# Taylor attention on one Trainium2 core: q's columns of two groups of heads in one projection, and the scores' constant one added by GpSimd instead of sums of values

## The chip, the core and the metric

The kernel runs on one core of a Trainium2 chip. The metric is the device time of one execution in microseconds (us). The kernel before took 3826.05 us, the median of three runs (3818.64 to 3838.03). Engines are named as the profile names them: PE (TensorE, matmuls; PEld is its weight load), DVE (VectorE), ACT (ScalarE), POOL (GpSimd), SP (SyncE, which issues the DMAs). SBUF is the memory that all engines work in, PSUM the one that PE writes to.

## What is computed

Two sublayers, each wrapped as x + LN(sublayer(LN(x))), in fp32, on x of shape 8 x 512 x 128 (8 batches, 512 tokens, 128 features). The change concerns the first sublayer, attention with 16 heads, 16 features per head for q and k and 64 for v, whose weights are a Taylor polynomial of second order in place of an exponential:

```python
def taylor_exp(x):
    x2 = (x[..., :, None] * x[..., None, :]).reshape(*x.shape[:-1], FEATURE_DIM * FEATURE_DIM) / R2
    return jnp.concatenate([ones, x / RRD, x2 / RD], axis=-1)
qf, kf = taylor_exp(q), taylor_exp(k)
A_qk = jnp.tril(jnp.einsum('bhnd,bhmd->bhnm', qf, kf))     # causal
y = jnp.einsum('bhnm,bhme->bhne', A_qk, v)
rms = jax.lax.rsqrt(jnp.mean(y * y, axis=-1, keepdims=True) + RMS_EPS)
y = y * rms * g_weight                                      # per head
out = y.transpose(0, 2, 1, 3).reshape(b, l, NUM_HEADS * HEAD_DIM) @ Wo.T
```

With s = q.k the weight is 1 + s/4 + s*s/32. Twice that is (1 + s/4)^2 + 1, and as y is normalised, the factor of two is taken up by the epsilon. The second sublayer is a stack of six layers of windowed attention and a gated feed-forward; nothing of it is changed.

## The kernel before

The program is one unrolled stream. PE's order is the order of the code (a manual schedule for PE); the other engines are ordered by a scheduler that works with priorities, and buffers come from pools with a fixed number of slots for each tag, so an instruction that writes a slot waits until the slot's last reader is done.

The Taylor attention comes first. Per batch there are 4 groups of 4 heads, and per group 3 steps (`STEPS`), which take the key blocks of 128 tokens as [0], [1] and [2, 3]; only queries from the block on are computed (512, 384, and 256 + 128 columns). `slot(k)` (L361) emits the work of step k: the scores of step k, then one of head norm, projection of q and k, or projection of v for a neighbouring group, once per batch some work on the next or last batch, and last the weighted sum of step k - 2.

- `project_qk` (L234): the 4 heads of a group have 16 features of q each, padded with 16 zero columns to 32 rows, so that every head stands in its own 32 rows of 128. Two matmuls of 128x512 (q and k), each copied out of PSUM by ACT (L240).
- `squares` (L260): per key block 4 matmuls (L270), one per head, each on its 32 rows of k and q, into two PSUM tiles; ACT squares them with bias 1 and scale 1/4 into `am` (L279). On the diagonal block of 128x128 alone, DVE adds one and multiplies by the causal mask `keep` (L283). Off the diagonal the one is not added.
- `in_by_features` (L211) makes the columns of x's normalised batch and, from the same PSUM tile, the running sums of x over the blocks before each block (`cb`, L221 to L223). `sums_before` (L226) multiplies them by v's weights: 8 matmuls of 128x4 (L230), copied by DVE to `vs` (L232). That is the sum of v over all earlier blocks, which is what a constant one off the diagonal adds to y.
- `weigh` (L289): y += v * am (L300) in one PSUM tile that has a single slot; after a group's last step DVE adds `vs` to y while it copies it out to `yT` (L308), and ACT squares that (L313).
- `head_norm` (L316) forms the mean squares with a matmul (`ms`, L321), and `attn_out` (L331) projects a batch's result (`po`, L336), normalises it and adds it to x, the sum on POOL (L345).

`am` lives in the tags `qk` and `v2`, two slots each; q and k in the tag `pe`; the scores in PSUM's tag `mm` (two slots, both taken by one step); projections, `ms`, `vs` and transposes share PSUM's tag `tr` (two slots). Then 192 units of the second sublayer follow, each 128 tokens of a batch in one layer. Before `by_keys` in every fourth of them from the sixth on (t = 5), `nc.tensor.addr_align(128, offset=IN_STEP)` (L747) pads PE's instruction stream with NOPs up to place 98 of 128.

Of the kernel before, what the change touches and what calls it, by code (L numbers as in the profile page):

```python
# [8 lines left out]
F32 = mybir.dt.float32  # L9
BF16 = mybir.dt.bfloat16  # L10
AF = mybir.ActivationFunctionType
ALU = mybir.AluOpType
AX = mybir.AxisListType
PSUM = bass.MemoryType.PSUM

P = 128
DM = 128
H = 16
FD = 16
HD = 64  # L20
# [8 lines left out]
def sandwich_kernel(ctx: ExitStack, tc: tile.TileContext, ins: dict, out: bass.AP):  # L29
    nc = tc.nc  # L30
    x_d = ins["L0_attn_hidden_states"]
    B, N, _ = x_d.shape
    NB = N // P
# [44 lines left out]
    def transposed(ps, src, rows, cols):  # L78
        nc.tensor.transpose(ps[:cols, :rows], src, ident[:rows, :rows])  # L79
# [58 lines left out]
    psum = ctx.enter_context(tc.tile_pool(name="psum", bufs=2, space=PSUM))  # L138
    wl = ctx.enter_context(tc.tile_pool(name="wl", bufs=2))
    f2 = ctx.enter_context(tc.tile_pool(name="f2", bufs=2))  # L140
    f3 = ctx.enter_context(tc.tile_pool(name="f3", bufs=3))
    f1 = ctx.enter_context(tc.tile_pool(name="f1", bufs=1))

    HF = HD // 2
    NP = H // 2
# [5 lines left out]
    def load_x(b):  # L151
        t = f2.tile([P, NP, W + P], F32, tag="kT", name=f"xin_{b}")
        xin[b] = t.rearrange("p a b -> p (a b)")[:, : NB * DM].rearrange("p (n d) -> p n d", d=DM)
        nc.sync.dma_start(xin[b], x_d[b].rearrange("(n p) d -> p n d", p=P))


    tw = wl.tile([P, 3, 2, 512], F32, tag="wqkv", name="tw")
# [6 lines left out]
    wqk = tw[:, 0]  # L164
    wvT = tw[:, 1].rearrange("p s c -> p (s c)")
# [28 lines left out]
    for qd in range(4):  # L194
        r = slice(qd * W, (qd + 1) * W)
# [6 lines left out]
    bt = [dict() for _ in range(B)]  # L202
    gr = [dict() for _ in range(NG)]
# [7 lines left out]
    def in_by_features(b):  # L211

        xl = bt[b].pop("xl")
        ps = psum.tile([P, NB, P], F32, tag="tr", name="tr")
        for j in range(NB):
            transposed(ps[:, j, :], xl[:, j, :], P, P)
        bt[b]["xlT"] = xlT = f2.tile([P, N], F32, tag="ge", name=f"xlT_{b}")
        nc.scalar.copy(xlT, ps.rearrange("p a b -> p (a b)"))
        cb = f2.tile([P, NB], F32, tag="cb", name=f"cb_{b}")
        nc.vector.memset(cb[:, 0:1], 0.0)  # L220
        nc.vector.tensor_reduce(cb[:, 1:NB], ps[:, : NB - 1, :], AX.X, ALU.add)  # L221
        for j in range(2, NB):
            nc.vector.tensor_tensor(cb[:, j : j + 1], cb[:, j : j + 1], cb[:, j - 1 : j], ALU.add)  # L223
        bt[b]["cb"] = cb

    def sums_before(b):  # L226

        ps = psum.tile([P, NP, NB], F32, tag="tr", name="vs")
        for c in range(NP):
            nc.tensor.matmul(ps[:, c, :], wvT[:, c * P : (c + 1) * P], bt[b]["cb"], start=True, stop=True)  # L230
        bt[b]["vs"] = vs = f2.tile([P, NP, NB], F32, tag="vs", name=f"vs_{b}")
        nc.vector.tensor_copy(vs, ps)  # L232

    def project_qk(G):  # L234
        b, g = divmod(G, NQ)
        gr[G]["qk"] = qk = f2.tile([P, 2, N], F32, tag="pe", name=f"tqk_{G}")
        for s in range(2):
            ps = psum.tile([P, N], F32, tag="tr", name="qk")
            nc.tensor.matmul(ps, wqk[:, s, g * P : (g + 1) * P], bt[b]["xlT"], start=True, stop=True)  # L239
            nc.scalar.copy(qk[:, s], ps)  # L240

    def project_v(G):
        b, g = divmod(G, NQ)
# [9 lines left out]

    STEPS = [[0], [1], [2, 3]]
    steps = [(G, s) for G in range(NG) for s in range(len(STEPS))]

    def squares(k):  # L260

        G, s = steps[k]
        qk = gr[G]["qk"]
        sc = [psum.tile([P, 2, N], F32, tag="mm", name="sc") for _ in range(2)]
        at_, places = 0, []
        for m in STEPS[s]:
            n = N - m * P
            for h in range(4):
                r = slice(32 * h, 32 * h + 32)
                nc.tensor.matmul(  # L270
                    sc[h // 2][:, h % 2, at_ : at_ + n],
                    qk[r, 1, m * P : (m + 1) * P], qk[r, 0, m * P :], start=True, stop=True,
                    skip_group_check=True,
                )
            places.append((m, at_, n))
            at_ += n
        am = f2.tile([P, 4, 512], F32, tag=("qk", "v2")[k % 2], name="am")
        for i in range(2):
            nc.scalar.activation(  # L279
                am[:, 2 * i : 2 * i + 2, :at_], sc[i][:, :, :at_], AF.Square, bias=1.0, scale=0.25  # L280
            )
        for m, o, n in places:
            nc.vector.scalar_tensor_tensor(  # L283
                am[:, :, o : o + P], am[:, :, o : o + P], 1.0,
                keep.unsqueeze(1).to_broadcast([P, 4, P]), ALU.add, ALU.mult,
            )
        gr[G]["am", s] = am, places

    def weigh(k):  # L289

        G, s = steps[k]
        b, g = divmod(G, NQ)
        if s == 0:
            gr[G]["y"] = psum.tile([P, 2, N], F32, tag="s", name="y", bufs=1)
        y, v = gr[G]["y"], gr[G]["v"]
        am, places = gr[G].pop(("am", s))
        for m, o, n in places:
            for h in range(4):
                r = slice(HD * (h % 2), HD * (h % 2 + 1))
                nc.tensor.matmul(  # L300
                    y[r, h // 2, m * P :], v[:, m, h * HD : (h + 1) * HD], am[:, h, o : o + n],
                    start=(m == 0), stop=(m == NB - 1), skip_group_check=True,
                )
        if s == len(STEPS) - 1:
            yT = f2.tile([P, 2, NB, P], F32, tag="sq", name="yT")
            with tc.high_priority():
                for i in range(2):
                    nc.vector.tensor_tensor(  # L308
                        yT[:, i], y[:, i].rearrange("p (n m) -> p n m", m=P),
                        bt[b]["vs"][:, 2 * g + i, :].unsqueeze(2).to_broadcast([P, NB, P]), ALU.add,  # L310
                    )
            ysq = f2.tile([P, 2, N], F32, tag="t1", name="ysq")
            nc.scalar.activation(ysq, yT.rearrange("p a n m -> p a (n m)"), AF.Square)  # L313
            gr[G]["yT"], gr[G]["ysq"] = yT, ysq

    def head_norm(G):  # L316
        yT, ysq = gr[G].pop("yT"), gr[G].pop("ysq")
        rs = f2.tile([P, 2, N], F32, tag="t2", name="rs")
        for i in range(2):
            ps = psum.tile([P, N], F32, tag="tr", name="ms")  # L320
            nc.tensor.matmul(ps, same, ysq[:, i], start=True, stop=True)  # L321
            ln = nc.scalar.activation(rs[:, i], ps, AF.Ln, bias=eps4, scale=1.0 / HD)
            issue_behind(ln, tables[-1])
        exps.append(nc.scalar.activation(rs, rs, AF.Exp, scale=-0.5))
        gr[G]["yn"] = yn = f1.tile([P, 2, N], F32, tag=("qT", "pT", "on", "oT")[G % NQ], name="yn")
        nc.vector.scalar_tensor_tensor(
            yn.rearrange("p a n -> p (a n)"), yT.rearrange("p a n m -> p (a n m)"), gw,
            rs.rearrange("p a n -> p (a n)"), ALU.mult, ALU.mult,
        )
# [31 lines left out]
    def slot(k):  # L361

        G, ph = divmod(k, len(STEPS))
        b, g = divmod(G, NQ)
        if k < len(steps):
            squares(k)
        if ph == 0 and 0 <= G - 2 < NG:
            head_norm(G - 2)
        if ph == 1 and G + 1 < NG:
            project_qk(G + 1)  # L370
        if ph == 2 and G + 1 < NG:
            project_v(G + 1)
        if g == 0 and ph == 1 and b + 1 < B:
            norm_in(b + 1)
        if g == 1 and ph == 0 and b + 1 < B:
            in_by_features(b + 1)
        if g == 1 and ph == 1 and b + 1 < B:
            sums_before(b + 1)
        if g == 1 and ph == 2 and b >= 1 and k < len(steps):
            attn_out(b - 1)  # L380
        if g == 2 and ph == 2 and b >= 1 and k < len(steps):
            to_state(b - 1)
        if 0 <= k - 2 < len(steps):
            weigh(k - 2)
# [339 lines left out]
    with tc.manual_schedule(engines={mybir.EngineType.PE}):  # L724
        norm_in(0)
        in_by_features(0)
        project_qk(0)
        project_v(0)
        sums_before(0)
        layers[0] = load_layer(0)  # L730
        for k in range(len(steps) + 2):
            slot(k)
# [83 lines left out]

def _attn_weights(given):

    import numpy as np

    parts = []
    for nm in ("Wq", "Wk"):
        w = given[f"L0_attn_{nm}"].reshape(H, FD, DM)
        parts.append(np.pad(w, ((0, 0), (0, FD), (0, 0))).reshape(2 * FD * H, DM).T)
    parts.append(given["L0_attn_Wv"].T)
    parts.append(given["L0_attn_Wo"].T.reshape(H // 2, P, DM).transpose(1, 0, 2).reshape(P, H // 2 * DM))
    return np.ascontiguousarray(np.concatenate(parts, 1))


# [39 lines left out]
```

## Time and profile before

| | |
|---|---|
| median of three runs | 3826.05 us |
| the profiled execution | 3825.62 us |
| its span, first to last instruction | 3823.9 us |
| granted PE clock, mean | 0.994 of full |
| PE busy | 3703.6 us, 97% |
| DVE, ACT, POOL busy | 73%, 70%, 48% |
| Taylor attention, with its start | about 0 to 535 us |
| scores' squares on ACT (L279), 128x1024 and 128x768 | 1.02 and 0.80 us each |
| masked add on DVE (L283) | 0.69 us each |
| q and k records on PE (L239) | 128, the shortest 0.59 us |
| records of the sums of values on PE (L230) | 128, 0.25 us each |

The page gives for each engine its busy time and for each group of equal instructions the number, the busy time, the mean duration of one, and the idle time ahead of them with what ended it. Matmuls overlap each other in the pipeline, so the time that a block of them takes on PE is read from the timeline, from its start to the next block's start, and not from the sum of its records. A line "A <- B" under the idle time names the instruction whose end released the waiting one.

### The profile page before, as it was taken

The page shows a single profiled execution, that of the slowest core. Times are in us where ns is not written, and L with a number is a line of the kernel's source. Part 1 is how long each engine was busy: PE and PEld are TensorE (multiplying, and loading weights), DVE is VectorE, ACT ScalarE, POOL GpSimd, SP SyncE. Part 2 cuts the span into 40 slices and gives each one's busy share as a digit, 9 for nine tenths or more (in the row PEclk, how much of TensorE's full clock was granted, in tenths as well). Part 3 has the DMA queues.
Part 4 walks back from the last instruction along what each step waited for, and adds up shares of the span by engine and source line. Part 5 has one row for each costly group of instructions (what it writes and reads, how often), then busy time and mean ns, then how long its engine had stood idle before and what let it go on. Part 6 is the DMA issues. An engine that isn't in the chain of part 4 may idle for free.

```text
span 3823.9 us, 152697 instructions
## 1 busy us (share of the span) xinstructions
PE 3703.6 (97%) x65600; PEld 2456.2 (64%) x65600; DVE 2794.7 (73%) x4308; ACT 2662.9 (70%) x6750; POOL 1842.6 (48%) x1311
## 2 busy tenths in 40 slices
PE   8999999999999999999999999999999999989997
PEld 4545556666666666666666666666666666666664
DVE  4555567787877778787777778777777878777774
ACT  5565557777777777777777777777777777767665
POOL 0000025555555555555555655555555555555552
PEclk9999999999999999999999999999999999999998
DMA  2000012222232222322222322223222222222221
GB/s 82 17 9 12 6 51 72 60 67 62 73 79 69 66 58 66 81 73 62 67 66 58 88 72 67 57 67 82 71 65 65 67 58 65 65 67 69 64 67 32
DMA packets 153219, 233.66 MB, mean 61 GB/s; under 512 B 32622, under 2 KB 53356, under 8 KB 151788
## 3 DMA queue, kind: packets, MB, share of 16 engines
q1 hardware_dynamic: 152556, 223.89, 22.8%
q8 instruction: 530, 8.68, 0.9%
q14 instruction: 133, 1.09, 0.1%
HBM read 24.54 MB, written 4.19 MB: 8 GB/s over the span
## 4 chain that ended last, share of the span: by engine, by line
PE 95%; issue 2%; ACT 2%; DVE 1%; POOL 0%; DMA 0%; POOLq 0%; SPq 0%; DVEq 0%; ACTq 0%
PE tr L79 20%; PE mm L439 17%; PE py L627 9%; PE mm L497 9%; PE po L598 8%; PE sp L558 8%; PE y L300 4%; PE mm L652 3%; PE mm L654 3%; PE py L687 3%; PE sc L270 3%; PE sp L551 2%; PE vv L248 2%; PE qk L239 1%; PE po L336 1%
## 5 line engine op out<-in xcount | busy, mean ns | idle before, releaser
L470 POOL TENSOR_TENSOR qk<-t,t 128x1024 f32<-128x1024 f32 x384 | 909.9, 2370 | 679.3 <-DVE t L454 405.3
L486 POOL TENSOR_TENSOR qk<-qk,ss 128x1024 f32<-128x1024 f32 x384 | 722.2, 1902 | 16.0
L439 PE MATMUL mm<-wqkv,state 128*128 128x512 f32 x1536 | 698.4, 597 | 2.6 <-ACT v L502 2.6
L447 DVE TENSOR_TENSOR t<-mm,tab 128x512 f32<-128x512 f32 x768 | 498.6, 671 | 239.5 <-PE mm L439 239.5
L570 ACT ACTIVATE pe<-sp,mx 128x64 f32<-128x64 f32 x3072 | 652.1, 381 | 2.3 <-DVE mx L566 2.3
L462 ACT ACTIVATE sq<-mm 128x512 f32<-128x512 f32 x768 | 421.3, 607 | 118.6 <-DVE t L454 114.0
L454 DVE TENSOR_TENSOR t<-mm,tab 128x1024 f32<-128x1024 f32 x384 | 468.4, 1220 | 5.9
L439 PEld LDWEIGHTS mm<-wqkv,state 128*128 128x128 f32 x1536 | 273.7, 191 | 289.6 <-issue 242.2
L473 DVE TENSOR_REDUCE ss<-sq 128x16 f32<-128x1024 f32 x384 | 448.6, 1209 | 0.7 <-ACT sq L462 0.6
L79 PE MATMUL tr<-ident,qk 128*128 128x128 f32 x3072 | 440.7, 276 | 1.8 <-ACT qT L536 0.8
L536 ACT COPY kT<-tr 128x512 f32<-128x512 f32 x384 | 225.6, 587 | 299.6 <-PE tr L79 299.4
L79 PEld LDWEIGHTS tr<-ident,qk 128*128 128x128 f32 x3072 | 351.0, 141 | 120.7 <-issue 100.8
L627 PE MATMUL py<-oT,wo 128*128 128x128 f32 x3072 | 377.4, 276 | 0.5 <-ACT oT L620 0.5
L627 PEld LDWEIGHTS py<-oT,wo 128*128 128x128 f32 x3072 | 364.5, 194 | 0.7 <-ACT oT L620 0.7
L497 PE MATMUL mm<-wqkv,state 128*128 128x512 f32 x768 | 363.1, 595 | 0.3 <-ACT sq L462 0.3
L620 ACT COPY oT<-tr 128x512 f32<-128x512 f32 x384 | 206.8, 589 | 221.5 <-PE tr L79 218.9
L598 PE MATMUL po<-v,pT 64*32 64x64 f32 x24576 | 301.9, 225 | 56.0 <-PE tr L79 49.1
L598 PEld LDWEIGHTS po<-v,pT 64*32 64x32 f32 x24576 | 274.2, 105 | 98.0 <-PE tr L79 88.5
L566 DVE TENSOR_REDUCE mx<-sp 128x16 f32<-128x1024 f32 x192 | 235.1, 1225 | 104.2 <-PE sp L558 104.2
L558 PE MATMUL sp<-kT,qT 64*32 64x64 f32 x24576 | 304.7, 226 | 6.4 <-issue 6.4
L558 PEld LDWEIGHTS sp<-kT,qT 64*32 64x32 f32 x24576 | 270.6, 105 | 62.5 <-issue 60.0
L606 DVE TENSOR_TENSOR on<-po,su 128x1024 f32<-128x1024 f32 x192 | 235.2, 1225 | 96.8 <-PE po L598 96.8
(114 smaller groups left out, 5082.8 us busy)
## 6 DMA issues: line engine op xcount, KB each, us to landing
v<-v SPq DMA_DIRECT2D x1152, 128.0 KB
v<-v SPq DMA_DIRECT2D x672, 64.0 KB
wqkv<-in_L_ffn_Wqkv_dram SPq DMA_DIRECT2D x6, 1536.0 KB
wo<-in_L_ffn_Wo_dram SPq DMA_DIRECT2D x6, 512.0 KB
xin<-_attn_hidden_states_dram SPq DMA_DIRECT2D x8, 256.0 KB
xr<-_attn_hidden_states_dram SPq DMA_DIRECT2D x8, 256.0 KB
x<-xr SPq DMA_DIRECT2D x8, 256.0 KB
xr<-x SPq DMA_DIRECT2D x8, 256.0 KB
```

What stands on the lines that cost most here:

```text
L79: nc.tensor.transpose(ps[:cols, :rows], src, ident[:rows, :rows])
L439: nc.tensor.matmul(ps[:, a].rearrange("p h d -> p (h d)"), lhs, wqkv[:, s, a, :], start=True, stop=True)
L447: nc.vector.tensor_tensor(t2[:, a], ps[:, 1 - a], tab[:, 2 * s + 1, j, HF * a : HF * (a + 1)].unsqueeze(1).to_broadcast([P, H, HF]), ALU.mult,
L454: nc.vector.tensor_tensor(t1, ps, tab[:, 2 * s, j, :].rearrange("p (a d) -> p a d", a=2).unsqueeze(2) .to_broadcast([P, 2, H, HF]), ALU.mult,)
L470: nc.gpsimd.tensor_tensor(qk[:, s].rearrange("p h a d -> p a h d"), t1, t2, ALU.add)
L473: su = nc.vector.tensor_reduce(u["ss"][:, s], u["sq", s].rearrange("p h a d -> p h (a d)"), AX.X, ALU.add)
L486: nc.gpsimd.tensor_tensor(t, t, ss[:, i, :].unsqueeze(2).to_broadcast([P, H, HD]), ALU.mult)
L497: nc.tensor.matmul(ps[:, p, :], lhs, L["wqkv"][:, 2, p, :], start=True, stop=True)
L558: nc.tensor.matmul(sp[W * w : W * (w + 1), p, pair, :], qT[HD * p : HD * (p + 1), pair, W * w : W * (w + 1)], kT[HD * p : HD * (p + 1), pa ...
L570: ex = nc.scalar.activation(pe[:, pair, p, :], sp[:, p, pair, :], AF.Exp, bias=mx[:, p, pair : pair + 1])
L598: nc.tensor.matmul(po[W * w : W * (w + 1), p, pair, :], pT[r, pair, W * w : W * (w + 1)], v2[r, w, HD * pair : HD * (pair + 1)], start=Tru ...
L627: nc.tensor.matmul(py, L["wo"][:, c, :], oT[:, c, :], start=(c == 0), stop=(c == NP - 1))
```

## The change

Three things are changed, all in the Taylor attention.

1. **q packed.** The rows of a q projection are no longer padded with zeros: 128 rows hold 8 heads, two in each 32 rows, and serve two groups. The zeros are now in k's weights: k of a group has its head's 16 rows in one half of its 32 and zeros in the other, so the product picks the right head. q is projected for even groups only, into a new pool `fq` with two slots, and the odd group uses the same tile. The heads are taken in another order (`heads`), for Wv and Wo too; their shapes stay.
2. **No sums of values.** `cb`, `sums_before` and `vs` go. After the last step DVE copies y out as one instruction of 128x1024.
3. **The one added to the scores.** Off the diagonal POOL adds 1.0 to the squares in place, behind ACT: 4 heads x 384, 256 and 128 columns for the key blocks 0, 1 and 2, one instruction each. DVE's masked add on the diagonal stays. The weighted sum waits for both.

```diff
+    fq = ctx.enter_context(tc.tile_pool(name="fq", bufs=2))
...
-        cb = f2.tile([P, NB], F32, tag="cb", name=f"cb_{b}")
-        nc.vector.memset(cb[:, 0:1], 0.0)
-        nc.vector.tensor_reduce(cb[:, 1:NB], ps[:, : NB - 1, :], AX.X, ALU.add)
-        for j in range(2, NB):
-            nc.vector.tensor_tensor(cb[:, j : j + 1], cb[:, j : j + 1], cb[:, j - 1 : j], ALU.add)
-        bt[b]["cb"] = cb
-
-    def sums_before(b):
-
-        ps = psum.tile([P, NP, NB], F32, tag="tr", name="vs")
-        for c in range(NP):
-            nc.tensor.matmul(ps[:, c, :], wvT[:, c * P : (c + 1) * P], bt[b]["cb"], start=True, stop=True)
-        bt[b]["vs"] = vs = f2.tile([P, NP, NB], F32, tag="vs", name=f"vs_{b}")
-        nc.vector.tensor_copy(vs, ps)
...
-        gr[G]["qk"] = qk = f2.tile([P, 2, N], F32, tag="pe", name=f"tqk_{G}")
-        for s in range(2):
+        k = f2.tile([P, 2, N], F32, tag="pe", name=f"tk_{G}")[:, 0]
+        q = fq.tile([P, N], F32, tag="tq", name=f"tq_{G}") if g % 2 == 0 else gr[G - 1]["q"]
+        gr[G]["q"], gr[G]["k"] = q, k
+        for s, dst in ((0, q), (1, k))[g % 2 :]:
+            cols = slice(g * P, (g + 1) * P) if s else slice(g // 2 * P, (g // 2 + 1) * P)
             ps = psum.tile([P, N], F32, tag="tr", name="qk")
-            nc.tensor.matmul(ps, wqk[:, s, g * P : (g + 1) * P], bt[b]["xlT"], start=True, stop=True)
-            nc.scalar.copy(qk[:, s], ps)
+            nc.tensor.matmul(ps, wqk[:, s, cols], bt[b]["xlT"], start=True, stop=True)
+            nc.scalar.copy(dst, ps)
...
-                    qk[r, 1, m * P : (m + 1) * P], qk[r, 0, m * P :], start=True, stop=True,
+                    tk[r, m * P : (m + 1) * P], tq[r, m * P :], start=True, stop=True,
...
                 keep.unsqueeze(1).to_broadcast([P, 4, P]), ALU.add, ALU.mult,
             )
+            if n > P:
+                nc.gpsimd.tensor_scalar(
+                    am[:, :, o + P : o + n], am[:, :, o + P : o + n], 1.0, None, ALU.add
+                )
...
-                for i in range(2):
-                    nc.vector.tensor_tensor(
-                        yT[:, i], y[:, i].rearrange("p (n m) -> p n m", m=P),
-                        bt[b]["vs"][:, 2 * g + i, :].unsqueeze(2).to_broadcast([P, NB, P]), ALU.add,
-                    )
+                nc.vector.tensor_copy(yT.rearrange("p a n m -> p a (n m)"), y)
...
-        if g == 1 and ph == 1 and b + 1 < B:
-            sums_before(b + 1)
...
-        sums_before(0)
...
+    heads = [8 * (g // 2) + 2 * r + g % 2 for g in range(H // 4) for r in range(4)]
+    wq = given["L0_attn_Wq"]
+    wk = given["L0_attn_Wk"].reshape(H, FD, DM)
+    k = np.zeros((H // 4, 4, 2, FD, DM), wk.dtype)
+    for i, h in enumerate(heads):
+        k[i // 4, i % 4, i // 4 % 2] = wk[h]
```

More of the change, by code (lines that the diff above doesn't have):

```diff
@@ L262, in squares @@
         G, s = steps[k]
-        qk = gr[G]["qk"]
+        tq, tk = gr[G]["q"], gr[G]["k"]
         sc = [psum.tile([P, 2, N], F32, tag="mm", name="sc") for _ in range(2)]
@@ L819, in _attn_weights @@
     import numpy as np
[L821 to L826, printed above, removed]
+    heads = [8 * (g // 2) + 2 * r + g % 2 for g in range(H // 4) for r in range(4)]
[4 more added lines that the diff above has]
+        k[i // 4, i % 4, i // 4 % 2] = wk[h]
+    wv = given["L0_attn_Wv"].reshape(H, HD, DM)[heads].reshape(H * HD, DM)
+    wo = given["L0_attn_Wo"].T.reshape(H, HD, DM)[heads]
+    parts = [
+        np.pad(wq, ((0, FD * H), (0, 0))).T,
+        k.reshape(2 * FD * H, DM).T,
+        wv.T,
+        wo.reshape(H // 2, P, DM).transpose(1, 0, 2).reshape(P, H // 2 * DM),
+    ]
     return np.ascontiguousarray(np.concatenate(parts, 1))
```

## The prediction, made before the changed kernel had run

> **What bounds the kernel now.** I read the page first: the span, the busy line, and the slices of PE (TensorE) and POOL (GpSimd).
>
> ```profile
> span 3823.9 us, 152697 instructions
> PE 3703.6 (97%) x65600; PEld 2456.2 (64%) x65600; DVE 2794.7 (73%) x4308; ACT 2662.9 (70%) x6750; POOL 1842.6 (48%) x1311
> ...
> PE   8999999999999999999999999999999999989997
> ...
> POOL 0000025555555555555555655555555555555552
> ```
>
> PE is busy almost everywhere; POOL does nothing in the first five and a half slices of 95.6 us. Those are the Taylor attention, the only stage that the change edits. The table by stage (columns: length; busy time and count of PE, PEld, DVE, ACT, POOL; PE clock; DMA share; GB/s) gives its limit:
>
> ```profile
> 0.00:60.00 60.00, 50.44 (x271) 25.52 (x272) 27.98 (x101) 27.87 (x42) 7.93 (x23) 0.94 0.43 130
> 60.00:535.00 475.00, 468.64 (x2929) 248.32 (x2929) 249.26 (x534) 274.75 (x393) 10.22 (x10) 0.99 0.03 10
> ```
>
> From 60 to 535 us PE idles 6.4 us of 475, DVE and ACT are busy for 52% and 58%, POOL for 2%. So work taken off PE here shortens the run, if no wait grows in its place. The timeline of one group (start, duration, engine, line, tiles, count) shows the order:
>
> ```profile
> 149.28 1.29 DVE L283 SCALAR_TENSOR_TENSOR am<-am,keep 128x512 f32<-128x512 f32 x2 [1.20 <-ACT am L279]
> 150.01 1.14 PE L270 MATMUL sc<-tqk 32*128 32x512 f32 x8
> 150.50 0.69 DVE L252 COPY tv<-vv 128x512 f32<-128x512 f32 x1
> 151.09 1.98 PE L321 MATMUL ms<-ysq,same 128*128 128x512 f32 x4
> ...
> 156.64 1.98 PE L239 MATMUL qk<-xlT,tw 128*128 128x512 f32 x4
> 156.74 1.51 ACT L279 ACTIVATE am<-sc 128x768 f32<-128x768 f32 x2 [0.75 <-PE sc L270]
> ...
> 158.79 1.95 PE L230 MATMUL vs<-cb,tw 128*128 128x4 f32 x16 [0.16 <-ACT tqk L240]
> 160.66 1.52 PE L300 MATMUL y<-am,tv 128*64 128x256 f32 x16
> 162.12 0.94 PE L270 MATMUL sc<-tqk 32*128 32x256 f32 x16
> 162.23 1.29 DVE L308 TENSOR_TENSOR yT<-y,vs 128x512 f32<-128x512 f32 x2 [1.26 <-PE y L300]
> 162.98 1.99 PE L248 MATMUL vv<-tw,xlT 128*128 128x256 f32 x8
> ```
>
> PE goes from one block to the next without a hole, in the order of the code. One fp32 matmul of the code is two MATMUL records.
>
> **PE, removed.** (a) q is projected for every second group only: 2 of 8 projections per batch, 16 in all. A pair takes 1.91 us from its start to the next block's (median of the warm pairs). Half of that is 0.96; four passes 0.43 us apart, of which two go, give 0.85. I take 0.9 for 15 of them. The first pair (21.43 to 25.14 us, at the low clock of the start) takes 3.71, so half of it goes, 1.85. Sum 15.4 (14.6 to 16.2). (b) The sums of values: 8 matmuls per batch, 16 records, 1.88 us from 158.79 to 160.66 and the same in each of 8 batches: 15.0. (c) The waits ahead of them for ACT's copy (0.16 in six batches, 0.11 in one): 1.1. Together **31.5 us** (30.7 to 32.3).
>
> **ACT and DVE, removed, at nothing.** 16 copies of 0.59 us on ACT; per batch a reduction of 0.55, two adds of 0.16 and a copy of 0.19 on DVE; two additions of 0.69 per group become one copy of 128x1024 from PSUM, which I put at 1.22 us from the row of the same size and source at L606 (1225 ns). None stands on the path while PE has work. Without that cover they would be a further gain.
>
> **A wait that moves up.** The scores of a step need ACT to have emptied the two buffers of the step before. Read off the timeline for all steps, the tightest place is the third step of a batch's third group: PE's first score comes 1.04 us and its third (the second buffer's) 0.88 us after ACT's two ends. There one projection, 0.96, goes from between. I charge 0.1 us in 7 batches, 0.5 with some latency. All other places keep over 1 us, and the long wait after the output projection (0.84 us, the second step of the third group) hangs on a chain of DVE, POOL and ACT that the change leaves as it is.
>
> **POOL, added.** Per group, 1536, 1024 and 512 elements per partition get their one: 96 instructions. No row shows this operation at this size. The rows of POOL's groups (busy, mean ns of one):
>
> ```profile
> L470 POOL TENSOR_TENSOR qk<-t,t 128x1024 f32<-128x1024 f32 x384 | 909.9, 2370 | 679.3 <-DVE t L454 405.3 <-PE tr L79 273.9
> L539 POOL COPY kT<-kT 128x256 f32<-128x256 f32 x144 | 57.1, 397 | 202.2 <-ACT kT L536 202.2
> L483 POOL TENSOR_SCALAR ss<-ss 128x32 f32<-128x32 f32 x192 | 54.7, 285 | 491.8 <-ACT ss L106 491.8
> ...
> L185 POOL MEMSET tri<- 128x256 f32 x1 | 0.3, 309 | 0.0
> ...
> L170 POOL MEMSET keep<- 128x128 f32 x1 | 0.2, 201 | 0.0
> ```
>
> Low end: the two memsets differ by 108 ns for 128 elements, 0.84 ns each; over L483's 285 ns for 32 that makes 1.55 us for 1536 elements. High end among big instructions: L470's strided two-input add, 2.31 ns each, 3.6 us. I take 1.6, 1.1 and 0.7 us (one input, nearest to L539 and L483): 3.4 us per group of about 14. What hides it: the weighted sum of a step stands two steps later on PE. From the end of ACT's second square to the first matmul of that sum, read off the timeline for all 96 steps, there are at least 5.95 us in the first two steps (typically 7.6 and 8.8) and typically 7.9 in the third (2.8 once); at most 1.9 of it goes with the removed work. Even 3.6 us fits. In POOL's queue the new instructions stand in step order; the residual add (L345, 1.27 us, waiting for DVE's `ao`) stands ahead of the third group's first step, whose scores end about when that add does, and one memset of `kT` waits for DVE at 315.0 us, before the next step's squares end. So nothing is held: 0 us.
>
> **PE's code, moved.** At t = 5 the code aligns PE's instruction stream to place 98 of 128 (L747). The trace shows the padding:
>
> ```profile
> L747 PEldq NOP  x45: 13/13/13, 605.5 to 608.7; - x45
> ```
>
> 80 matmuls go, of 4 instructions each (two loads, two passes), and 5 semaphore waits (counted in the built programs): 325 fewer, 69 modulo 128. So 45 paddings become 114. The 45 took 3.25 us, 72 ns each, while PE worked off the 16 transposes and projections already queued; the next block began at 609.8, 1.1 us after the last. 69 more cost 5.0, less about 1.0 of cover: **+4.0 us**, once. If one costs only its own 13 ns, they are 0.9 and hidden: 0. Later alignments start from the same place as now. [...]
>
> **Sum.** -31.5 + 0.5 + 0 + 4.0 = -27.0 us. The profiled execution took 3825.62 us (span 3823.9 and 1.7 around it), 0.4 below the median of three, 3826.05. Predicted: **3798.6 us**, 0.7% less.
>
> **Rivals.** *DVE held by POOL.* The new adds start together with DVE's masked add on the same tile (both wait for ACT). DVE's add has two SBUF inputs. Beside POOL memsets it took 684 and 693 ns against 682 to 694 alone, but no row has it beside a POOL instruction that reads, so I bound it: held for the whole of POOL's third-step add (0.7 to 1.2 us), the copy of v at 150.50 ends at 151.9 to 152.4, and the second `ms` matmul, due at 151.94 in the same PSUM slot, waits 0 to 0.5 us. At 0.35 in 32 groups it gives 11 us: 3810 (3803 to 3815). [...]
>
> [...]
>
> *POOL becomes the bound (slower).* If all of L483's 285 ns beyond the 103 ns of a one-element memset belonged to its 32 elements, one element costs 5.7 ns: 3072 of them and three starts are 17.8 us per group, 570 us for 32 groups, where the stage now takes 535: 3825.6 + 35 = 3860. It decides from about 5.4 ns per element (535/32 = 16.7 us per group). Against it: the big two-input adds stay under 2.4 ns, the one-input copy of 256 elements under 1.6.
>
> *The change does not do what it says:* the sums were hidden anyway, 3826. Against it: they stand in PE's own order with no hole around them.
>
> **Chances.** Forecast (3790 to 3806) 0.66, of this 0.06 for hidden paddings, 3795; DVE held 0.14; the code's place 0.12; hidden anyway 0.04; POOL the bound 0.04. Half a per cent, 19 us, is about what a measurement of this kernel can tell (its three runs span 3818.64 to 3838.03), so the line is at 3807. Faster: the forecast, a third of the second case and half of the third: 0.77; same 0.19; slower 0.04. Range 3788 to 3816: below, the largest removal with hidden paddings (3825.6 - 32.3 - 0.8 = 3792.5) less a few us of the runs' own spread; above, the DVE case's end.
>
> **What would show it.** Right: no L230 records, 96 q and k records of 0.59 us instead of 128 on PE, the first FFN block some 31 us earlier, POOL's add of 1536 elements near 1.6 us, no wait of `y` on POOL, DVE's masked add still 0.69 us, 114 paddings and a hole of about 4 us on PE at t = 5. Wrong: PE waiting for POOL at `y`, masked adds of over 1 us, or an attention stage shortened by much less than 31 us.

## The result: slower by 0.7%, where 0.7% faster was forecast

The changed kernel took 3853.28 us, the median of six runs (3845.24 to 3860.9); beside it the kernel before took 3826.73. The ratio is 1.0066, 95% interval [1.0043, 1.0089]. Its profiled execution, the longest of the six, took 3860.9 us; the one of before took 3825.62. The page of the changed kernel, the lines that answer to those of before:

```profile
span 3859.2 us, 152682 instructions
PE 3707.8 (96%) x65440; PEld 2453.1 (64%) x65440; DVE 2865.4 (74%) x4236; ACT 2655.3 (69%) x6734; POOL 2146.0 (56%) x1407
...
PE   8999989999999999999999999999999999999997
...
POOL 6555555555565555555555655555555555555452
```

PE has 160 records fewer and yet is busy 4 us longer. POOL is now at least half busy in the first six slices too. The table by stage of the changed kernel (columns as in the table of before):

```profile
0.00:60.00 60.00, 49.49 (x256) 23.05 (x256) 36.03 (x89) 31.70 (x46) 40.16 (x33) 0.97 0.44 130
60.00:552.00 492.00, 458.71 (x2782) 234.85 (x2782) 311.64 (x474) 262.74 (x374) 281.83 (x96) 0.97 0.03 10
```

PE idles 33 us of 492 where it idled 6 of 475, its granted clock is 0.97 where it was 0.99, and DVE is busy 312 us where it was 249, although instructions were taken from it. POOL's groups of the changed kernel, each form by itself, up to 552 us (busy, mean ns of one, idle time ahead and what ended it):

```profile
L278 POOL TENSOR_SCALAR am<-am 128x1536 f32<-128x1536 f32 x32 | 145.8, 4555 | 64.6 <-ACT am L269 46.5 <-ACT ln_rs L106 18.1
L278 POOL TENSOR_SCALAR am<-am 128x1024 f32<-128x1024 f32 x32 | 95.7, 2992 | 4.6 <-ACT am L269 3.6 <-POOL am L278 0.6 <-DVE yn L316 0.4
L278 POOL TENSOR_SCALAR am<-am 128x512 f32<-128x512 f32 x32 | 62.9, 1965 | 90.2 <-ACT am L269 74.1 <-issue 16.2
```

4.6, 3.0 and 2.0 us, where the prediction took 1.6, 1.1 and 0.7. DVE's groups of the changed kernel from 60 us on, and after them four of before (60 to 535 us):

```profile
L273 DVE SCALAR_TENSOR_TENSOR am<-am,keep 128x512 f32<-128x512 f32 x115 | 99.6, 887 | 81.0 <-ACT am L269 69.2 <-issue 11.8
L316 DVE SCALAR_TENSOR_TENSOR yn<-yT,vec,rs 128x1024 f32<-128x1024 f32 x30 | 62.4, 2080 | 43.5 <-ACT rs L314 43.5
L243 DVE COPY tv<-vv 128x512 f32<-128x512 f32 x56 | 38.1, 681 | 6.2 <-PE vv L239 6.2
L127 DVE TENSOR_SCALAR xs<-xr,ln_mv,ln_rs 128x128 f32<-128x128 f32 x28 | 37.1, 1602 | 0.0
L301 DVE COPY yT<-y 128x1024 f32<-128x1024 f32 x30 | 36.6, 1218 | 9.3 <-PE y L294 9.1
L127 DVE TENSOR_SCALAR ao<-po,ln_mv,ln_rs 128x128 f32<-128x128 f32 x28 | 9.6, 405 | 4.2 <-ACT ln_rs L106 4.2
```
```profile
L283 DVE SCALAR_TENSOR_TENSOR am<-am,keep 128x512 f32<-128x512 f32 x116 | 77.7, 690 | 88.1 <-ACT am L279 87.7
...
L252 DVE COPY tv<-vv 128x512 f32<-128x512 f32 x56 | 38.5, 688 | 18.7 <-PE vv L248 18.7
L326 DVE SCALAR_TENSOR_TENSOR yn<-yT,vec,rs 128x1024 f32<-128x1024 f32 x30 | 38.5, 1284 | 28.2 <-ACT rs L324 28.1
...
L127 DVE TENSOR_SCALAR xs<-xr,ln_mv,ln_rs 128x128 f32<-128x128 f32 x28 | 7.8, 343 | 0.0
```

The same instructions got longer: `xs`, the normalisation of the state's input, from 343 to 1602 ns, `yn` from 1284 to 2080, the masked add from 690 to 887. The copies out of PSUM did not: `tv` took 681 (688 before), although 36 of its 56 ran beside one of POOL's adds. `ao`, the same instruction as `xs` with its source in PSUM, took 405 (404 before), but none of its 28 ran beside an add, so it tells nothing. The timeline of the changed kernel shows where this reaches PE (start, duration, engine, line, tiles, count, idle time ahead):

```profile
106.44 7.29 POOL L278 TENSOR_SCALAR am<-am 128x1536 f32<-128x1536 f32 x2 [2.59 <-ACT ln_rs L106]
...
106.93 5.40 DVE L127 TENSOR_SCALAR xs<-xr,ln_mv,ln_rs 128x128 f32<-128x128 f32 x4
...
111.11 1.99 PE L239 MATMUL vv<-tw,xlT 128*128 128x256 f32 x8
112.25 1.63 DVE L127 TENSOR_SCALAR xl<-xin,ln_mv,ln_rs 128x128 f32<-128x128 f32 x4
113.80 1.26 DVE L316 SCALAR_TENSOR_TENSOR yn<-yT,vec,rs 128x1024 f32<-128x1024 f32 x1
...
115.59 1.21 DVE L301 COPY yT<-y 128x1024 f32<-128x1024 f32 x1
116.72 0.68 DVE L243 COPY tv<-vv 128x512 f32<-128x512 f32 x1
...
117.45 1.11 PE L79 MATMUL tr<-ident,xs 128*128 128x128 f32 x4 [4.35 <-DVE tv L243]
...
118.50 3.68 PE L294 MATMUL y<-am,tv 128*64 128x512 f32 x8
```

This is a batch's third group. Beside 7.29 us of POOL, four `xs` take 5.40 us in place of 1.11. DVE's chain behind them is late, at its end the copy of v (`tv`), whose PSUM slot PE's transposes of the state need: PE idles for 4.35 us. The first block of y after it then takes 3.68 us in place of 1.94, at a granted clock of 0.50 (stretch, its length, PE busy, granted clock, DMA share, GB/s):

```profile
117.40:122.20 4.80, 4.75 (x16) 0.50 0.00 0
```

Seven such holes, one per batch from the second on, make 26.5 us. The clock fell to half behind six of them, not behind one of 2.99 us; and before has two such stretches of 3.4 us, at 293 and 426 us (granted clock 0.55 and 0.53), without a hole of over 0.7 us ahead of them. What makes the clock fall is not shown.

The starts of the FFN's units split the loss. Against the profile of before, unit 0 starts 17.5 us later (31 earlier was forecast), unit 6 28.7, unit 164 27.9, and the end is 35.2 later. The 17.5 are, with PE's overlapping records counted once: 30.6 us of matmuls taken away, 27.9 us more idle time, and 20 us more for matmuls that were not changed (y 10.2, scores 5.4, `ms` 3.6, others 1.0). By an estimate from each kind's median, about two thirds of these 20 us lie in the stretches at half clock.

### The profile page after: what moved, and what is told of

Same layout as the page of the kernel before. It is cut to its first block, busy times and chain, and to the rows that moved or that the text cites. A ratio compares the mean times of both kernels' runs of the same rounds, so it can differ in the third digit from the quotient of the medians.

```text
span 3859.2 us, 152682 instructions
## 1 busy us (share of the span) xinstructions
PE 3707.8 (96%) x65440; PEld 2453.1 (64%) x65440; DVE 2865.4 (74%) x4236; ACT 2655.3 (69%) x6734; POOL 2146.0 (56%) x1407
## 3 DMA queue, kind: packets, MB, share of 16 engines
q14 instruction: 135, 1.11, 0.1%
## 4 chain that ended last, share of the span: by engine, by line
PE 91%; DVE 4%; issue 2%; ACT 2%; POOL 0%; DMA 0%; POOLq 0%; SPq 0%; DVEq 0%; ACTq 0%
PE tr L79 20%; PE mm L427 17%; PE py L615 9%; PE mm L485 9%; PE po L586 8%; PE sp L546 8%; PE mm L640 3%; PE mm L642 3%; PE py L675 3%; PE y L294 3%; PE sp L539 2%; PE sc L260 2%; PE po L326 2%; PE vv L239 1%; PE qk L230 1%
## 5 line engine op out<-in xcount | busy, mean ns | idle before, releaser
L278 POOL TENSOR_SCALAR am<-am 128x1536 f32<-128x1536 f32 (+2 forms) x96 | 303.9, 3171 | 159.5 <-ACT am L269 124.2
L586 PE MATMUL po<-v,pT 64*32 64x64 f32 x24576 | 303.0, 226 | 59.3 <-PE tr L79 48.5
L471 POOL TENSOR_SCALAR ss<-ss 128x32 f32<-128x32 f32 x192 | 54.7, 285 | 491.6 <-ACT ss L106 491.6
```

Of the source, the lines that this page charges most:

```text
L586: nc.tensor.matmul(po[W * w : W * (w + 1), p, pair, :], pT[r, pair, W * w : W * (w + 1)], v2[r, w, HD * pair : HD * (pair + 1)], start=Tru ...
```

## The experiments

**Theory 1:** POOL's add keeps DVE's instructions waiting, those that read and write SBUF alone, and DVE's lateness reaches PE in the third group. Its rivals: y waits for POOL's sums themselves; the packing of q costs something; the place of PE's code takes the gain. The table has all runs but e12. The ratio is to before's median on the same chip (3825.92 to 3837.03 us), so a time is to be compared only with the one beside it. The starts of the units (counted from 0) are those of one profiled execution each, in us against before's profile:

| kernel | ones added by | NOPs at t = 5 | ratio to before | unit 0 | unit 6 | unit 164 | end |
|---|---|---|---|---|---|---|---|
| after | POOL | 114 | 1.0066 [1.0043, 1.0089] | +17.5 | +28.7 | +27.9 | +35.2 |
| e1 | none, sums kept | 109 | 0.9991 [0.9977, 1.0004] | -11.3 | -0.3 | -1.8 | +4.4 |
| e2 | POOL, one column | 114 | 0.9945 [0.9927, 0.9963] | -28.7 | -18.1 | -18.7 | -10.4 |
| e3 | POOL, into scratch | 45 | 1.0107 [1.0081, 1.0132] | +43.4 | +45.8 | +45.3 | +46.1 |
| e4 | DVE | 4 | 0.9942 [0.9922, 0.9961] | -15.7 | -9.3 | -7.3 | -11.2 |
| e5 | DVE in third group | 115 | 0.9983 [0.9974, 0.9993] | -16.3 | -7.1 | -8.2 | -11.0 |
| e6 | POOL in third group | 3 | 1.0033 [1.0019, 1.0048] | +14.7 | +21.4 | +20.4 | +5.9 |
| e7 | POOL, one column | 124 | 0.9937 [0.9921, 0.9954] | -26.7 | -20.2 | -20.7 | -16.8 |
| e8 | ACT and DVE | 4 | 0.9976 [0.9966, 0.9987] | -4.8 | -2.0 | -3.2 | -7.8 |
| e9 | DVE | 45 | 0.9958 [0.9943, 0.9973] | -16.1 | -15.1 | -14.5 | -10.6 |
| e10 | POOL, one column | 45 | 0.9934 [0.9917, 0.9952] | -26.6 | -26.1 | -26.1 | -17.5 |
| e11 | POOL, state later | 108 | 1.0052 [1.0035, 1.0070] | +12.5 | +22.0 | +22.4 | +25.5 |
| e13 | DVE | 4 | 0.9953 [0.9939, 0.9966] | -13.7 | -7.7 | -8.0 | -8.8 |
| e14 | DVE | 45 | 0.9958 [0.9944, 0.9972] | -16.1 | -15.4 | -16.1 | -9.9 |
| e15 | DVE, state later | 5 | 0.9933 [0.9918, 0.9948] | -22.4 | -16.9 | -15.9 | -22.4 |

### What POOL's adds do

**e1_q_packed**: the kernel before with the packing of q alone (the lines of `project_qk`, `squares` and the weights from the diff).

> Only the packing of q: one q projection for two groups, k's weights with the zeros, the heads reordered. The sums of values stay, POOL adds nothing. [...] Theory 2 (the removed PE work was no gain, other engines set the pace of the stage): no change or slower, 3826 or more.

3830.44 us where before took 3837.03: 6.6 less, short of the 8 to 14 that theory 1 made of it (15.4 for q, less what the paddings cost), with an interval that includes no change. The stage gave 11.3 of the 15.4 us forecast for q; the run-in of the FFN (unit 0 to 6), with 109 NOPs in it, took 10.9 back. So the packing is not what costs; whether the code's place is comes further down.

**e2_one_column**: the changed kernel, with the adds' work taken away but not their instructions (most of the ones are left out of its result).

```diff
-                    am[:, :, o + P : o + n], am[:, :, o + P : o + n], 1.0, None, ALU.add
+                    am[:, :, o + P : o + P + 1], am[:, :, o + P : o + P + 1], 1.0, None, ALU.add
```

> The changed kernel, but POOL adds its one to a single column per head (4 elements in place of 1536, 1024 and 512), so most of the ones are left out of the computation. All instructions, waits and paddings of the changed kernel stay. Theory 1: the stage is shortened as was forecast, by 31 us; 114 paddings and what follows them cost 8 to 10: about 3803 to 3806. Theory 2 (not POOL's work, but the new waits, the packing or the order of the instructions cost the time): near the changed kernel, 3850.

3813.84 us against 3837.03. `xs` is back at 342 ns, the masked add at 690, and the stage is 28.7 us shorter: nearly the 31 that the prediction had without POOL. PE's groups up to unit 0, first of the changed kernel, then of this one:

```profile
L294 PE MATMUL y<-am,tv 128*64 128x512 f32 (+3 forms) x1024 | 169.8, 465 | 3.5 <-DVE yT L301 3.0 <-POOL am L278 0.5
...
L311 PE MATMUL ms<-ysq,same 128*128 128x512 f32 x124 | 66.4, 640 | 3.7 <-DVE tv L243 3.5 <-DVE state L349 0.3
...
L79 PE MATMUL tr<-ident,xs 128*128 128x128 f32 x28 | 5.3, 316 | 26.5 <-DVE tv L243 26.5
```
```profile
L294 PE MATMUL y<-am,tv 128*64 128x512 f32 (+3 forms) x1024 | 158.8, 442 | 1.2 <-DVE yT L301 1.2
...
L79 PE MATMUL tr<-ident,xs 128*128 128x128 f32 x28 | 4.6, 286 | 0.0
```

In the changed kernel y waits 0.5 us for POOL's `am` in the whole stage. The sums are in time; it is the transposes that wait, and for DVE.

**e3_scratch**: the kernel before, with POOL's add put in, its result written to a tile that nobody reads.

```diff
+            if n > P:
+                scr = fs_.tile([P, 4, 384], F32, tag="scr", name="scr")
+                nc.gpsimd.tensor_scalar(
+                    scr[:, :, : n - P], am[:, :, o + P : o + n], 1.0, None, ALU.add
+                )
```

> The kernel before, with POOL adding one to the same elements of the squares, but into a scratch tile that nobody reads; sums and projections stay. No matmul waits for POOL's result; only slots are freed later. Theory 1: the adds hold DVE all the same; the stage of the changed kernel is 49 us longer than the removed work allows, so about 45 to 55 us above before, 3870 to 3880, with the normalisation of xs at over 1 us per instruction. Theory 3 (the weighted sum waits for POOL's result): nothing waits here, 3827.

3875.27 us, 38 more than before on that chip (45 to 55 were expected), with nothing of PE's work or code changed and nobody waiting for the result. Its lines of `xs` (60 to 552 us) and of the transposes (up to 550 us):

```profile
L127 DVE TENSOR_SCALAR xs<-xr,ln_mv,ln_rs 128x128 f32<-128x128 f32 x27 | 36.8, 1648 | 0.0
```
```profile
L79 PE MATMUL tr<-ident,xs 128*128 128x128 f32 x24 | 4.5, 314 | 21.9 <-DVE tv L253 21.9
```

`yn` takes 2000 ns. So the loss needs neither adds that are late for y nor the edits on PE.

**e12_pool_alone**: POOL's and DVE's adds by themselves, behind the last output of the kernel before; it ran once.

```diff
+                for i in range(2):
+                    for n in (384, 256, 128):
+                        nc.gpsimd.tensor_scalar(big[:, :, :n], big[:, :, :n], 1.0, None, ALU.add)
...
+                for i in range(2):
+                    nc.gpsimd.tensor_scalar(big, big, 1.0, None, ALU.add)
+                for i in range(24):
+                    nc.vector.tensor_scalar(
+                        own[:, i % 4, :], own[:, i % 4, :], b2_c[:, 0:1], g_c[:, 0:1], ALU.subtract, ALU.mult
+                    )
```

> The kernel before, with a measurement put behind its last output: GpSimd's add of one in place on 1536, 1024 and 512 elements, twice, with VectorE idle; then the same on VectorE with GpSimd idle; then two of GpSimd's largest beside 24 of VectorE's normalisations (128x128). [...] Theory 1b (GpSimd is slow at this by itself): about 4.5, 3.0 and 1.5 us alone too, and VectorE's normalisation is still held from 0.34 to over 1 us beside it. The time is some 40 us longer than before and says nothing.

Its groups and then its timeline, from 3824 us on:

```profile
L717 POOL TENSOR_SCALAR big<-big 128x1536 f32<-128x1536 f32 x2 | 8.2, 4092 | 0.2
...
L717 POOL TENSOR_SCALAR big<-big 128x1024 f32<-128x1024 f32 x2 | 5.5, 2769 | 0.2
L717 POOL TENSOR_SCALAR big<-big 128x512 f32<-128x512 f32 x2 | 3.0, 1490 | 0.2
L720 DVE TENSOR_SCALAR big<-big 128x1536 f32<-128x1536 f32 x2 | 1.9, 960 | 20.5 <-POOL big L717 20.5
```
```profile
3849.16 9.21 DVE L725 TENSOR_SCALAR own<-own,vec 128x128 f32<-128x128 f32 x7
3849.21 8.25 POOL L723 TENSOR_SCALAR big<-big 128x1536 f32<-128x1536 f32 x2 [4.91 <-DVE own L721]
```

Both halves of theory 1b hold. POOL is slow alone: (4092 - 1490)/1024 = 2.54 ns per element and 0.19 us. In the stage it took 4.56 us for 4.09 alone, so it is held too, but little: 31 of the 32 largest adds started there while DVE's masked add ran, and of those of 1024 elements nine of the ten that did took 3.28 us, the others mostly 2.8. And DVE is held for longer: in the 8.25 us of POOL's two adds and 0.2 us after, DVE got through four normalisations, which take 0.33 us each when POOL is idle; single ones lasted up to 4.21 us, where POOL's instruction took 4.09. Not all of DVE is held: in the changed kernel `xs`, from SBUF to SBUF, took 1602 ns for 343, while `tv`, which reads PSUM, took 681 for 688. Why the one is held and the other is not, no run shows.

### Where it costs

**e5_third_on_dve** and **e6_third_on_pool**: the changed kernel with DVE in the third group alone, and with POOL there alone.

```diff
-                nc.gpsimd.tensor_scalar(
+                eng = nc.vector if G % NQ == 2 else nc.gpsimd
+                eng.tensor_scalar(
```

> The changed kernel, with the adds of one on VectorE in the third group of heads of each batch alone; GpSimd keeps those of the other three groups. Theory 1, sharpened (GpSimd's add holds VectorE's instructions, and that costs only where VectorE's work is on TensorE's path: in the third group, where the input norm of the state, the transposes and the copy of v meet): most of the loss comes back, PE's idle time between 60 and 500 us falls from 27 us to 8-12, time 3817 to 3831 us, with the paddings still in (115 NOPs). Rival 4 (each held instruction costs wherever it stands, so each group bears a quarter): a quarter of some 40 us comes back, 3840 to 3848 us, idle time about 22 us.

> The complement: GpSimd adds only in the third group of heads of each batch, VectorE in the other three. Theory 1, sharpened: nearly the whole loss of the stage is there, PE's idle time between 60 and 500 us 25 us or more, time 3835 to 3845 us (few paddings: 3 NOPs at the fifth unit, so it misses the 8 us that the changed kernel pays there). Rival 4 (a quarter each): 3818 to 3825 us, idle time 16 to 19 us.

e5 took 3821.13 us, e6 3840.57 (before 3825.92). Both as the sharpened theory had it: in e5's stage 24 of 32 groups have POOL's adds, and it starts the FFN as early as e4 (16.3 and 15.7 us ahead), although `yn` is held in it (1904 ns). e6 has 8 groups with POOL and nearly the whole loss. Its line of the transposes, up to 547 us:

```profile
L79 PE MATMUL tr<-ident,xs 128*128 128x128 f32 x28 | 6.4, 371 | 26.5 <-DVE tv L243 26.5
```

The same 26.5 us as with POOL everywhere. A held instruction costs where DVE has no slack left, and elsewhere little: with POOL's adds in the other 24 groups, PE waits as in e4 (5.5 us of the transposes for `tv`), but for 5.5 in place of 3.9 us of `ms` for `tv`. A kernel with adds in the third group alone, on DVE, was not run.

**e11_state_later**: the changed kernel with one step moved in PE's order.

```diff
-        if g == 2 and ph == 2 and b >= 1 and k < len(steps):
+        if g == 3 and ph == 1 and b >= 1 and k < len(steps):
             to_state(b - 1)
```

> The changed kernel, GpSimd's adds and all, with one step moved: the transposes of the state (to_state) stand two steps later in TensorE's order, in the second step of the fourth group in place of the last of the third. Theory 1, sharpened (GpSimd only makes VectorE late, and the transposes pass that on because they need the PSUM that v's copy frees): TensorE has other work while VectorE catches up; the 23 us of idle time and the half clock behind it go, time 3822 to 3832 us with the paddings in. Rival 7 (the hole moves to the next that needs that copy, the mean squares of the heads one step on): at most 8 us come back, 3845 to 3853 us.

3850.37 us where before took 3829.9: about as slow. The hole moved, as the rival had it, though to another place than it named:

```profile
L294 PE MATMUL y<-am,tv 128*64 128x512 f32 (+3 forms) x1024 | 166.2, 457 | 26.6 <-DVE yT L301 26.3 <-POOL am L278 0.3
...
L79 PE MATMUL tr<-ident,xs 128*128 128x128 f32 x28 | 4.6, 287 | 1.3 <-ACT tq L231 1.3
```

The next y needs the copy `yT` of the last, which stands in DVE's queue just ahead of `tv`. DVE itself was late, not the step's place wrong.

### The place of PE's code

From unit 0 to 6 the changed kernel's PE stalls for "issue" three times by over 0.5 us, by 1.01 in unit 2 and by 4.05 and 2.08 in unit 5; before has one such stall, of 0.82. The changed kernel's paddings, and PE's two stalls near them in the timeline:

```profile
L734 PEldq NOP  x520: 13/13/13, 626.4 to 3233.5; - x174
```
```profile
634.99 1.80 PE L79 MATMUL tr<-ident,pe 128*128 128x128 f32 x8 [4.05 <-issue]
...
643.68 0.42 PE L586 MATMUL po<-v,pT 64*32 64x64 f32 x21 [2.08 <-issue]
```

The first 114 of the 520 stand from 626.4 to 634.8 us. The hole of 4.05 us is the forecast one, but the clock of 634 to 640 us is 0.72 after it, and a second stall follows. e2 (114 NOPs) has the same pair: 4.07 and 1.89.

**e7_one_column_aligned**: e2 with `nc.tensor.addr_align(128, offset=55)` ahead of `norm_in(0)`.

> The one-column kernel (GpSimd adds one to one column of four heads, most ones left out, 3813.8 us) with TensorE's code shifted by an alignment ahead of its first instruction, where TensorE waits 7.6 us for data anyway, so that the alignment at the fifth unit wants about 10 NOPs in place of 114. Nothing else differs. If the 8 to 10 us that three kernels with 109 to 114 NOPs lost from the fifth to the sixth unit come from those paddings and what follows them: 3803 to 3807 us, and the unit starts no later than at the fifth, against the kernel before. Rival 5 (that loss has another cause, as the shorter stage meeting the FFN's first transfers): 3812 to 3816 us, the loss still between the fifth and sixth unit.

3805.17 us against 3825.92 falls in the expected range but shows nothing: with this offset t = 5 wants 124 NOPs, not the 10 that were meant, and 6.5 us are lost from unit 0 to 6. The next two have the right offsets (24 for e4's code, 6 for e2's), so that 45 NOPs are wanted as in the kernel before:

> The kernel with all adds on VectorE, and 87 NOPs ahead of TensorE's first instruction (an alignment; TensorE waits 7.6 us for data there, 87 NOPs took some 6.3 us), so that the FFN's code lies as in the kernel before against steps of 128 instructions, and the alignment at the fifth unit wants 45 NOPs again. Without it this kernel lost 6.4 us between the start of the first and the sixth unit, with issue stalls of 0.87 and 2.26 us. If the place of the code does that (theory 5a): the stalls fall to the one of 0.8 us of the kernel before, nothing is lost up to the sixth unit, and the ratio to before falls from 0.994 to about 0.9925 (3797 to 3799 us where before takes 3826). Rival 5 (the loss comes from the shorter stage meeting the FFN's first work otherwise): stalls as they were, ratio 0.994.

> The one-column kernel with 69 NOPs ahead of TensorE's first instruction, for the same purpose: the alignment at the fifth unit wants 45 NOPs, as before, in place of 114. Theory 5a: the 10.5 us lost between the first and the sixth unit stay, the sixth unit starts 27 to 29 us ahead of before, ratio 0.9925 or less. Rival 5: the sixth unit stays at 18 us ahead, ratio 0.9945.

From unit 0 to 6 e9 loses 0.9 us and e10 0.5, where e4 and e2 lost 6.4 and 10.5; e9's only stall for issue over 0.5 us in that stretch is one of 0.79. So this loss is one of the code's place, as theory 5a said; why a place makes PE stall no run shows. But the ratios hardly moved, where 0.9925 was expected of both. Side by side on one chip:

> The kernel with all adds on VectorE once more, as the partner of the next two on one chip: ratio 0.994, as before.

> The same with 87 NOPs ahead of TensorE's first instruction, beside its partner. If the 6 us that it keeps from the first to the sixth unit reach the end: 5 to 7 us below the partner. If the last layers' own issue stalls (between 0.5 and 13.5 us in the profiles so far) take them back: within 2 us of it.

3812.97 us for the kernel with 4 NOPs, 3815.72 for the placed one. At unit 164 the placed one is 8 us ahead, at the end 1. The last layer, whose units are no longer aligned, took it back, in part by its own issue stalls (PE idle for issue from unit 164 on: 0.5 us in e6, 8 in e4 and e13, 11 in e14, 12 in before, 13.5 in e9). Between e13 and e14 they make 3 of the 7 us; what decides them, and where the rest went, stays open.

### Who else can add

**e4_dve_adds**: the changed kernel with `nc.vector` in place of `nc.gpsimd`.

> The changed kernel with the same 96 adds on DVE instead of POOL; POOL idles again in the stage. Theory 1: DVE reads without a competitor; from xl's 343 ns for 128 elements out of SBUF against 404 out of PSUM an element costs about 0.5 ns, so 2.4 us more per group on an engine that had 6.6 us free: no hole, 4 paddings at t = 5 in place of 114, 31 us below before, about 3795 to 3800. Rival: DVE itself becomes late with 20% more work, its copies of v hold PE as in the changed kernel: 3820 or more.

3813.25 us against 3837.03, faster than before and than the changed kernel; 24 us came of the 31 expected. The same adds take 0.95, 0.69 and 0.42 us on DVE; 5.5 us of waits of the transposes for `tv` are left.

**e8_act_first**: e4 with the largest add on ACT, `nc.scalar.add(far, far, 1.0)` in the first step.

> The kernel with all adds on VectorE (3813.3 us), but the largest add of each group (1536 elements, 0.95 us on VectorE) put on ScalarE, behind its squares. If what that kernel still lacks of the one-column kernel's stage (13 us) is VectorE's 2.1 us a group: 3800 to 3808 us, waits for VectorE's copy of v near zero. Rival 6 (ScalarE is then late: its add of some 1.3 us stands ahead of the next squares and of the logarithms): 3813 to 3825 us, PE waiting for ScalarE's am or rs.

3818.33 us against 3825.92: worse than e4, as rival 6 had it. PE waits 6.1 us for ACT's `am` ahead of the scores between 60 and 500 us.

**e15_dve_adds_state_later**: e4 with e11's edit.

> The kernel with all adds on VectorE, with the transposes of the state two steps later as in the run that did so with GpSimd's adds. There the wait went over to the copy of y (20 us of it), because VectorE itself was late by the length of GpSimd's instructions. Here VectorE is late by its own 2 us a group: if the step's place costs at that size, the 5.5 us of waits for v's copy go and 4 to 6 us with them, against the partner; if the wait moves again, the same time.

3803.99 us, ratio 0.9933 [0.9918, 0.9948], 9 less than its partner e13: the best that was run with the whole computation. Its lines up to 550 us:

```profile
L294 PE MATMUL y<-am,tv 128*64 128x512 f32 (+3 forms) x1024 | 158.8, 442 | 3.2 <-DVE yT L301 3.2
...
L79 PE MATMUL tr<-ident,xs 128*128 128x128 f32 x28 | 4.6, 286 | 1.0 <-ACT tq L231 1.0
```

Of the 5.5 us for `tv` nothing is left. The same edit that moved a hole of 4 us hides one of 1 us, presumably because DVE has caught up two steps later.

## Why the prediction was wrong

- **PE, removed: 31.5 us: right but for 2 us.** e2's stage is 28.7 us shorter, where 31.0 was forecast with the scores' 0.5 (0.6 by e2's lines). Of the rest, 1.8 us are waits of `ms` for DVE's copy of the state (0.1 of waits before), which the prediction did not have. The copy of y took 1.218 us (1.22 forecast).
- **POOL, added, "So nothing is held: 0 us": the step that failed.** The sum looked at who waits for POOL's result, and there it was right (0.5 us of waits). It put nothing for what DVE does meanwhile, which it left to a rival. That cost some 46 us: the difference between e2 and the changed kernel at unit 0 (28.7 + 17.5), and 46 by their ratios (1.0066 less 0.9945, times 3827).
- **The add's size** fell with it. 0.84 ns per element came from two memsets, which do not read; alone it takes 2.54. The line through e12's rows gives 0.19 + 32 x 0.00254 = 0.27 us for L483's 32 elements, whose 285 ns the prediction had in hand and split between start and elements from the memsets. Of the bounds, the high end (3.6 us, from the two-input add) was nearest and itself too low.
- **The rival "DVE held by POOL", priced at 11 us,** had the mechanism, and was given 0.14. Its price failed twice: it took the hold to be one short add in the third step, and it put the damage at the copy of v in all 32 groups. What is held is any of `xs` (1602 ns for 343), `xl` (585 for 344), `yn` (2080 for 1284) and the masked add (887 for 690), DVE's instructions between SBUF tiles that ran beside POOL's, `xs` for up to 4.11 us; and the damage is in the third group, where `xs`, `xl`, `yn`, `yT` and `tv` follow each other on DVE. Before, DVE waited only 0.45 us for PE ahead of that `tv` (119.95 us in its timeline): this was the slack to read. To the 28 us of waits PE's slower matmuls, by the estimate above about two thirds of it at half clock, added 20.
- **The rival "POOL becomes the bound"** named 3860 us, near what came, by chance: it took 5.7 ns per element and POOL busy all the time. The add takes 2.54 alone, and POOL was busy for 282 of 492 us.
- **PE's code, moved: +4.0 us: the count and the hole right (114, 4.05 us), the sum not.** A second stall and the low clock made it 7.7 us from unit 5 to 6, and 11.2 from unit 0 to 6. That the end would keep it isn't shown: e13 and e14 differ by 2.8 us the other way. The 0.8 us at the low end of the range and the 0.12 for the code's place were the author's estimates, and the changed kernel's profile shows neither a gain of 0.8 us nor what sets such stalls: up to unit 6 it has stalls for issue of 1.01, 4.05 and 2.08 us, where before has one of 0.82.
- **The rest** of the profiled execution's 62 us beyond the forecast (48.5 in the stage, 7 in the run-in) is 6.6 us behind unit 6, all in the last layer, which varies: from unit 164 to the end, e4 and e13, the same kernel, differ by 3.1 us.

## What to carry to other kernels

Before work goes to an idle POOL, list what DVE does between SBUF tiles at that time: each of these may wait about as long as POOL's instruction takes (in e12 one of 0.33 us lasted 4.21 beside adds of 4.09), and the price was set here where DVE's chain had the least slack (26.5 us of PE's waits in the third group), not by POOL's share of busy time. Short pieces, or a place beside DVE's reads of PSUM, might lower it; neither was tried. Here DVE itself did it in about a quarter of the time (0.96 us for 4.09, e12). A wait of PE cost more than its length where the clock fell behind it: after one of 4.35 us the next block took 3.68 us in place of 1.94, at a clock of 0.50.

## What the runs showed of the hardware that was not expected

- On POOL a `tensor_scalar` of 512 elements took 1.49 us, a copy of the same size 0.62 (e12); DVE did the former in 0.43.
- NOPs that should do nothing take 72 ns each in the stream before (45 from 605.5 to 608.7 us) and 74 in the changed kernel (114 from 626.4 to 634.8). By the former e9's 87 are an estimated 6.3 us ahead of its first matmul, where before waits 7.59 us for data. And in the first FFN units PE stalls for issue by up to 2.3 us at a time, or by none over 0.5 us (e10), according to where the code lies.
